# Parts of the next chunk's convolution among the copies of a turned write pass

## Chip, cores and metric

The kernel runs on one core of one Trainium2 chip, as one launch. The metric is the device time in microseconds (us); less is better. Engines are named PE (TensorE), DVE (VectorE), ACT (ScalarE), POOL (GpSimd) and SP (SyncE, which here only issues DMAs).

## What is computed

Two layers follow one another on a picture batch of 8 x 128 x 128 pixels with 128 channels. Layer 0 is a linear attention with a layer norm. Layer 1 is a two-dimensional selective scan; its first half is what this document is about. Cut to that:

```python
xz = x @ Win
xb, z = jnp.split(xz, 2, axis=-1)                 # 256 channels each
xb = conv3x3_depthwise(xb, conv_w)                # 9 taps for each channel
xb = silu(xb + conv_b)
xf = xb.reshape(Bb, Cd, L)                        # pixels in natural order
xt = transpose_of_h_and_w(xb).reshape(Bb, Cd, L)  # pixels in turned order
xs = stack([xf, xf[..., ::-1], xt, xt[..., ::-1]])
x_dbl = einsum('bcl,cd->bdl', xs_flat, Wxproj)    # 8 rows of dt, one of B, one of C
```

A scan over the 16384 pixels of each image and direction follows, and then a gate, a norm and a projection. The scan needs its input both in natural and in turned order.

## The kernel before

Three stages run one after the other: layer 0, `layer1_front` and `layer1_scan`. A barrier of all engines stands before the last. The change is in `layer1_front` alone.

**Chunks and images.** The front works on 8 images, one after the other, each in 16 chunks of 8 x 128 = 1024 pixels. The 256 channels are two halves of 128 partitions, c = 0 and c = 1. Step n handles chunk n (g is its number within the image), and parts of n + 1 and n + 2. The tile `ures` (128 x 2 x 16384, fp32) holds the whole image after the convolution; there is only one of it.

**One chunk.** For each half c:
- `project` (L476) multiplies the input with `Win` on PE into the PSUM tile `pxb`, of which there is one. `place` (L484) copies it with ACT into `xb`, with the edge columns of the neighbouring chunks.
- The nine taps of the convolution are spread over four engines. `taps_pe` (L500) does two of them, as eight matmuls into the PSUM accumulator `acc`, of which there are two. `taps_act` (L508) does three as scaled copies on ACT; POOL adds the second and the third to the first. `taps_dve` (L520) adds these three to `acc` (L522) and does the last four taps there (L524).
- `silu` (L528) writes the result from `acc` to `ures` on ACT, which frees that `acc`.

Then `rows` (L533) makes the ten rows of dt, B and C on PE, `sum_d` (L580) keeps a running sum of the directions for the skip term, `keep_rows` and `spread` (one step later) bring B to all partitions, and `by_b` (L554) multiplies the chunk in `ures` with it on DVE and writes it out in natural order.

**The write pass.** When an image is complete, `leave` (L627) writes it in turned order. It has 32 copies, k = 0 to 15 for c = 0 and k = 16 to 31 for c = 1. Each reads an eighth of the rows over all columns of `ures` into a 4 KB-per-partition tile `turned` (L635) and sends it off by a DMA of 512 KB (L636). The copies with k % 5 equal to 1 or 3 are on ACT, the others on DVE: ACT has 1, 3, 6, 8, 11, 13, 16, 18, 21, 23, 26, 28 and 31. After k = 9 and k = 19 `split` (L611) turns five of the ten rows with PE, copies them with ACT (`xh`, L619), cuts them on DVE into bf16 parts (L44, L46) and sends these off (L625). A next image's chunk can't overwrite a half of `ures` before all the copies of that half have read it.

**Buffers.** Copies with k % 3 equal to 2 use the two buffers of the tag "tc". The others use the four buffers of the tag "tb", in turn with `xh`, the two `parts` tiles of each split, the second and third tile of each `taps_act`, and `sum_d`'s tile. Each takes the buffer that the fourth allocation before it had, and waits until its last reader, mostly a DMA, is done.

**Order.** `in_order` keeps every engine's instructions, and SP's DMAs, in the order in which the program is written: an instruction that waits holds all behind it on its engine. At an image's boundary (`before and g == 0`; n = 16, 32, ... 112, and n = 128 at the end), step n has these parts: taps_dve(n,0), keep_rows, project and place of (n+1,1), taps_pe(n,1), the DMAs of load and store_sum, spread, by_b(n-1), the pass, load_sum, taps_act(n+1,0), silu(n,0), taps_pe(n+1,0), project(n+2,0), taps_dve(n,1), taps_act(n+1,1), silu(n,1), place(n+2,0), rows(n), sum_d(n). So the accumulator of (n,0) is ready before the pass and is read after it.

Of the kernel before, what the change touches and what calls it, by code (L numbers as in the profile page):

```python
# [40 lines left out]
def split3(nc, parts, x):  # L41

    for j in range(3):
        nc.vector.tensor_copy(parts[j], x)  # L44
        if j < 2:
            nc.vector.tensor_tensor(x, x, parts[j], ALU.subtract)  # L46
# [338 lines left out]
def layer1_front(ctx: ExitStack, tc, x1, win, conv_w, conv_b, wxp, d_par, ubs, xds, xps, gts, gs):  # L385
# [23 lines left out]
    def tap(dw, dh):  # L409
        return 3 * (dh + 1) + dw + 1  # L410
# [51 lines left out]
    def place_of(n):  # L462
        return SEQ[n // NCH % B], n % NCH
# [3 lines left out]
    def load(n):  # L467
        b, g = place_of(n)
        x = xins[n % 2]
        cols = CW + 1 if g < NCH - 1 else CW  # L470
        src = x1[b].rearrange("c (w h) -> c w h", h=H)[:, g * CW : g * CW + cols, :]
        nc.sync.dma_start(x[:, 0:cols, inner], src)
        if g == NCH - 1:
            nc.gpsimd.memset(x[:, CW, :], 0.0)

    def project(n, c):  # L476
        pxs[n, c] = px = pj.tile([P, CW, H], F32, name="pxb", tag="pj")
        for hf in range(2):
            nc.tensor.matmul(  # L479
                px[:, hf * 4 : hf * 4 + 4, :], wi[:, c, :], xins[n % 2][:, hf * 4 : hf * 4 + 4, inner],  # L480
                start=True, stop=True,
            )

    def place(n, c):  # L484

        g = n % NCH
        xb, old = xbs[n % 2], xbs[(n - 1) % 2]
        nc.scalar.copy(xb[:, c, 1 : CW + 1, inner], pxs.pop((n, c)))  # L488
        if g == 0:
            nc.gpsimd.memset(xb[:, c, 0, :], 0.0)  # L490
        else:
            nc.scalar.copy(old[:, c, CW + 1, inner], xb[:, c, 1, inner])
            nc.scalar.copy(xb[:, c, 0, inner], old[:, c, CW, inner])
        if g == NCH - 1:
            nc.gpsimd.memset(xb[:, c, CW + 1, :], 0.0)

    def at(n, c, dw, dh):
        return xbs[n % 2][:, c, 1 + dw : 1 + dw + CW, 1 + dh : 1 + dh + H]

    def taps_pe(n, c):  # L500
        accs[n, c] = acc = pa.tile([P, CW, H], F32, name="acc", tag="acc")
        for hf in range(2):
            s = slice(hf * 4, hf * 4 + 4)
            for j, (dw, dh) in enumerate(ON_PE):
                x = xins[n % 2][:, hf * 4 + dw : hf * 4 + dw + 4, 1 + dh : 1 + dh + H]
                nc.tensor.matmul(acc[:, s, :], wt[:, j, c, :], x, start=(j == 0), stop=(j == len(ON_PE) - 1))  # L506

    def taps_act(n, c):  # L508
        for j, d in enumerate(ON_ACT):
            if j:  # L510
                t = wp.tile([P, CW, H], F32, name="tap", tag="tb", bufs=4)
            else:
                t = wp.tile([P, CW, H], F32, name="tap", tag="ta", bufs=2)
            nc.scalar.activation(t, at(n, c, *d), AF.Copy, scale=cw[:, c, tap(*d) : tap(*d) + 1])  # L514
            if j:
                nc.gpsimd.tensor_tensor(sums[n, c], sums[n, c], t, ALU.add)  # L516
            else:
                sums[n, c] = t

    def taps_dve(n, c):  # L520
        acc = accs[n, c]
        nc.vector.tensor_tensor(acc, sums.pop((n, c)), acc, ALU.add)  # L522
        for d in ON_DVE:
            nc.vector.scalar_tensor_tensor(  # L524
                acc, at(n, c, *d), cw[:, c, tap(*d) : tap(*d) + 1], acc, ALU.mult, ALU.add
            )

    def silu(n, c):  # L528
        g = n % NCH
        u = ures[:, c, g * CH : g * CH + CH]  # L530
        nc.scalar.activation(u, accs.pop((n, c)).rearrange("p w h -> p (w h)"), AF.Silu, bias=cb[:, c : c + 1])  # L531
# [10 lines left out]
    def keep_rows(n):  # L542
        b, g = place_of(n)
        t = xdt[n % 2]
        nc.scalar.copy(t[0:64, :], prs.pop(n))
        for hf in range(2):
            s = slice(g * CH + hf * 512, g * CH + hf * 512 + 512)
            nc.sync.dma_start(xds[b][:, s], t[32 * hf : 32 * hf + R + 2, :])

    def spread(n, hf):  # L550
        pbs[n, hf] = p = pm.tile([P, 1, 512], F32, name="pb", tag="m")
        nc.tensor.matmul(p[:, 0, :], bsel[:, hf, :], xdt[n % 2], start=True, stop=True)

    def by_b(n):  # L554

        b, g = place_of(n)
        dst = ubs[b, NAT].rearrange("c p l -> p c l")
        for hf in range(2):
            s = slice(g * CH + hf * 512, g * CH + hf * 512 + 512)
            u = ures[:, :, s]  # L560
            nc.vector.tensor_tensor(u, u, pbs.pop((n, hf)).to_broadcast([P, NC2, 512]), ALU.mult)
            nc.sync.dma_start(dst[:, :, s], u)
# [8 lines left out]
    def load_sum(n, c):  # L571
        b, g = place_of(n)
        if b // 2 != 2:
            gls[n, c] = gl = wp.tile([P, CH], F32, name="gl", tag="d", bufs=2)
            if b // 2 == 0:
                nc.sync.dma_start(gl.rearrange("p (e q) -> p e q", e=NCH), gts[b % 2, c, :, :, g])
            else:
                nc.sync.dma_start(gl, sums_at(n, c))
# [21 lines left out]
    def store_sum(n, c):  # L600
        nc.sync.dma_start(sums_at(n, c), dus.pop((n, c)))
# [4 lines left out]
    def load_rows(b, i):  # L606
        r = slice(i * half, i * half + half)
        xws[b, i] = x = wp.tile([P, half, H], F32, name="xw", tag="d", bufs=2)
        nc.sync.dma_start(x, xds[b].rearrange("r (w h) -> w r h", h=H)[:, r, :])

    def split(b, i):  # L611

        r = slice(i * half, i * half + half)
        x = xws.pop((b, i))
        pt = pj.tile([P, half, P], F32, name="ptx", tag="pj")
        for j in range(half):
            nc.tensor.transpose(pt[:, j, :], x[:, j, :], ident)
        y = wp.tile([P, half, W], F32, name="xh", tag="tb", bufs=4)
        nc.scalar.copy(y, pt)  # L619
        for order, v in ((TURN, y), (NAT, x)):  # L620
            q = wp.tile([P, 3, half, P], BF16, name="parts", tag="tb", bufs=4)
            split3(nc, [q[:, j] for j in range(3)], v)
            dst = xps[b, order].rearrange("j r (a e) -> a j r e", e=P)
            for j in range(3):
                nc.sync.dma_start(dst[:, j, r, :], q[:, j])  # L625

    def leave(b):  # L627

        for i in range(2):
            load_rows(b, i)  # L630
        for k in range(NC2 * NCH):
            c, i = divmod(k, NCH)
            t = wp.tile([P, CW, W], F32, name="turned", tag="tc" if k % 3 == 2 else "tb", bufs=2 if k % 3 == 2 else 4)
            copy = nc.scalar.copy if k % 5 in (1, 3) else nc.vector.tensor_copy
            copy(t, uturn[:, c, i * CW : i * CW + CW, :])  # L635
            nc.sync.dma_start(ubs[b, TURN][c][:, i * CH : i * CH + CH], t.rearrange("p h w -> p (h w)"))  # L636
            if k % 10 == 9 and k < 20:
                split(b, k // 10)

    def step(n):  # L640

        live, then, later, before = 0 <= n < N, 0 <= n + 1 < N, 0 <= n + 2 < N, 1 <= n <= N
        b, g = place_of(n)
        if live:
            taps_dve(n, 0)
        if before:
            keep_rows(n - 1)
        if then:
            project(n + 1, 1)
            place(n + 1, 1)  # L650
        if live:
            taps_pe(n, 1)
        if later:
            load(n + 2)
        if before:
            for c in range(NC2):
                store_sum(n - 1, c)
        if live and g != 0:
            for c in range(NC2):
                load_sum(n, c)  # L660
        if before:
            for hf in range(2):
                spread(n - 1, hf)
        if before and g == 0:
            by_b(n - 1)
            leave(place_of(n - 1)[0])
        if live and g == 0:
            for c in range(NC2):
                load_sum(n, c)
        if then:  # L670
            taps_act(n + 1, 0)
        if live:
            silu(n, 0)
        if then:
            taps_pe(n + 1, 0)
        if later:
            project(n + 2, 0)
        if live:
            taps_dve(n, 1)
        if then:  # L680
            taps_act(n + 1, 1)
        if before and g != 0:
            by_b(n - 1)
        if live:
            silu(n, 1)
        if later:
            place(n + 2, 0)
        if live:
            rows(n)
            sum_d(n)  # L690
# [522 lines left out]
```

## Time and profile before

| | us |
|---|---|
| three runs: lowest, median, highest | 9591.18, 9600.28, 9600.95 |
| the profiled execution | 9596.25 |
| its span, from the first to the last instruction | 9594.5 |
| DVE busy in it | 8167.1 (85%) |
| ACT busy | 7164.4 (75%) |
| POOL busy | 7188.9 (75%) |
| PE busy | 6323.6 (66%) |

The sums over the whole span mix the stages. Cut at the stages' limits, the trace shows:

```profile
0.00:2300.00 2300.00, 2081.91 (x9222) 1280.35 (x9223) 1472.88 (x2564) 1359.70 (x2343) 1125.27 (x1255) 0.98 0.30 113
2300.00:2640.00 340.00, 302.00 (x799) 126.50 (x798) 268.57 (x240) 273.93 (x346) 198.58 (x115) 0.96 0.46 159
2640.00:4845.00 2205.00, 1640.44 (x4087) 634.19 (x4085) 1911.06 (x1654) 1741.43 (x1982) 1531.92 (x669) 0.89 0.78 255
4845.00:9594.00 4749.00, 2299.27 (x10086) 1103.17 (x10248) 4514.58 (x4211) 3789.29 (x3586) 4333.16 (x2323) 0.62 0.70 205
```

Each line is a window of the span (us from its start) and its length, then the busy time of PE, PE's weight loads, DVE, ACT and POOL with the number of instructions, and at the end the clock that TensorE was granted (1.00 is full), the share of time that the DMA engines were busy, and the GB/s that they moved. The first line is layer 0, the last the scan. The second is the start of the front up to the end of its first image, the third the rest of the front: eight write passes and seven images.

The transfers of the front that matter here, from the page (tile written and read, queue, number, size):

```profile
ubs<-ures SPq DMA_DIRECT2D x256, 512.0 KB
ubs<-turned SPq DMA_DIRECT2D x256, 512.0 KB
```

The copies of the pass have these durations in the trace: DVE x152 with a median of 1026 ns, ACT x104 with 1924 ns.

### The profile page before, as it was taken

What the parts mean: (1) busy time and instruction counts of PE and PEld (TensorE: products, weight loads), DVE (VectorE), ACT (ScalarE), POOL (GpSimd) and SP (SyncE); (2) the same over time, 40 slices, a digit from 0 to 9 for tenths busy, and PEclk for the clock granted to TensorE, in tenths of its full rate; (3) what the DMA queues carried; (4) which work ended last, traced back from release to release, by engine and by line L of the source; (5) the groups of instructions that cost most, each with busy time, mean ns of one, the idle gap of its engine ahead of it and who ended that gap; (6) DMA issues with size and microseconds to landing.
All of it is one profiled execution on the core that took longest, in us unless ns stands there. A gap on an engine that the chain in (4) does not pass through costs nothing. (4 is left out here: it accounts for less than half of the span.)

```text
span 9594.5 us, 89820 instructions
## 1 busy us (share of the span) xinstructions
PE 6323.6 (66%) x24190; PEld 3144.2 (33%) x24352; DVE 8167.1 (85%) x8668; ACT 7164.4 (75%) x8256; POOL 7188.9 (75%) x4361
## 2 busy tenths in 40 slices
PE   8999998988977788777823544636345363543636
PEld 5555655554322233222300311304023040220403
DVE  6667765563988899888989999999999999999996
ACT  5556565566877788777878888887887888788785
POOL 3445544455665578776859999998998999999897
PEclk9999999999988899888955755757556575665857
DMA  2332233313476678987765957769486685867858
GB/s 91 133 133 83 92 132 132 132 75 135 172 262 233 227 262 248 266 264 265 248 199 166 271 164 216 229 177 263 150 237 203 185 259 164 242 190 198 242 165 212
DMA packets 1034807, 1851.21 MB, mean 193 GB/s; under 512 B 274852, under 2 KB 500772, under 8 KB 1026112
## 3 DMA queue, kind: packets, MB, share of 16 engines
q1 hardware_dynamic: 999488, 1711.23, 54.2%
q0 software_dynamic: 34816, 134.23, 7.1%
q8 instruction: 199, 3.26, 0.1%
q14 instruction: 304, 2.49, 0.1%
HBM read 1153.03 MB, written 692.12 MB: 192 GB/s over the span
## 5 line engine op out<-in xcount | busy, mean ns | idle before, releaser
L892 POOL TENSOR_TENSOR ubt<-ubt,sp 128x1024 f32<-128x1024 f32 x1024 | 2457.5, 2456 | 197.3 <-ACT sp L885 107.8
L881 PE MATMUL px<-rows,dtw 128*128 128x512 bf16 x1893 | 914.6, 576 | 2259.8 <-DVE y L951 1032.6
L516 POOL TENSOR_TENSOR tap<-tap 128x1024 f32<-128x1024 f32 x512 | 1206.0, 2366 | 634.7 <-ACT tap L514 511.8
L524 DVE SCALAR_TENSOR_TENSOR acc<-xb,cw,acc 128x1024 f32<-128x1024 f32 x1024 | 1320.7, 1290 | 52.7 <-ACT tap L514 0.9
L885 ACT ACTIVATE sp<-px 128x1024 f32<-128x1024 f32 x1024 | 1044.2, 1024 | 398.3 <-PE px L881 244.5
L958 POOL TENSOR_TENSOR y<-y,ubt 128x512 f32<-128x512 f32 x768 | 1164.2, 1568 | 138.0 <-DVE ubt L932 135.1
L506 PE MATMUL acc<-xi,wt 128*128 128x512 f32 x2048 | 953.9, 609 | 384.6 <-ACT ures L531 384.2
L881 PEld LDWEIGHTS <-dtw 128*128 128x128 bf16 x2048 | 164.8, 110 | 3054.1 <-issue 951.5
L889 ACT ACTIVATE px<-sp,sa 128x1024 f32<-128x1024 f32 x1024 | 1110.2, 1109 | 6.1
L899 DVE TENSOR_TENSOR_SCAN ubt<-px,state,ubt 128x1024 f32<-128x1024 f32 x480 | 1106.2, 2336 | 6.6 <-issue 4.9
L901 DVE TENSOR_TENSOR_SCAN ubt<-px,state,ubt 128x1024 f32<-128x1024 f32 x480 | 1105.0, 2336 | 6.5 <-issue 4.7
L514 ACT ACTIVATE tap<-xb,cw 128x1024 f32<-128x1024 f32 x768 | 834.0, 1139 | 68.4 <-POOL tap L516 67.9
L885 ACT ACT_TABLE_LOAD x512 | 656.9, 1283 | 185.3 <-PE px L881 149.8
L282 POOL TENSOR_TENSOR q<-q,qs 128x512 f32<-128x512 f32 x256 | 271.2, 1060 | 642.2 <-DVE qs L281 642.2
L506 PEld LDWEIGHTS acc<-xi,wt 128*128 128x128 f32 x2048 | 383.9, 192 | 929.8 <-ACT ures L531 486.7
L889 ACT ACT_TABLE_LOAD x512 | 656.9, 1283 | 9.1
L1023 PEld LDWEIGHTS px<-wg,z 128*128 128x128 f32 x4096 | 586.7, 229 | 132.2 <-issue 126.4
L1023 PE MATMUL px<-wg,z 128*128 128x128 f32 x4096 | 585.6, 312 | 0.0
L915 PE MATMUL pc<-rows,csel 128*128 128x512 bf16 x1017 | 516.3, 588 | 100.8 <-DVE rstd L1011 91.8
L479 PE MATMUL pxb<-xi,wi 128*128 128x512 f32 x1024 | 495.9, 606 | 4.3 <-ACT xb L488 4.3
L951 DVE TENSOR_TENSOR y<-y,px 128x1024 f32<-128x1024 f32 x384 | 468.6, 1220 | 14.2
L298 ACT ACTIVATE sq<-o 128x512 f32<-128x512 f32 x256 | 161.2, 630 | 423.0 <-DVE o L296 421.8
(158 smaller groups left out, 15369.2 us busy)
## 6 DMA issues: line engine op xcount, KB each, us to landing
ubt<-ubs SPq DMA_DIRECT2D x512, 1024.0 KB
zs<-z SPq DMA_DIRECT2D x512, 256.0 KB
ubs<-ures SPq DMA_DIRECT2D x256, 512.0 KB
ubs<-turned SPq DMA_DIRECT2D x256, 512.0 KB
z<-zs SPq DMA_DIRECT2D x256, 512.0 KB
y<-gs POOLq DMA_DIRECT2D x128, 1024.0 KB, 12.0
rows<-xps SPq DMA_DIRECT2D x1536, 60.0 KB
xi<-x SPq DMA_DIRECT2D x120, 576.0 KB
```

Source lines behind the costliest of these rows:

```text
L506: nc.tensor.matmul(acc[:, s, :], wt[:, j, c, :], x, start=(j == 0), stop=(j == len(ON_PE) - 1))
L514: nc.scalar.activation(t, at(n, c, *d), AF.Copy, scale=cw[:, c, tap(*d) : tap(*d) + 1])
L516: nc.gpsimd.tensor_tensor(sums[n, c], sums[n, c], t, ALU.add)
L524: nc.vector.scalar_tensor_tensor(acc, at(n, c, *d), cw[:, c, tap(*d) : tap(*d) + 1], acc, ALU.mult, ALU.add)
L881: nc.tensor.matmul(p[:, hf * 512 : hf * 512 + 512], sl.dw[:, c * P : c * P + P], src, start=True, stop=True)
L885: nc.scalar.activation(t, da[n, c], AF.Softplus)
L889: nc.scalar.activation(da[n, c], sp[n, c], AF.Exp, scale=sa[:, sl.s, c : c + 1])
L892: nc.gpsimd.tensor_tensor(ubt[n][:, c, :], ubt[n][:, c, :], sp.pop((n, c)), ALU.mult)
L899: nc.vector.tensor_tensor_scan(e[:, ::-1], x[:, ::-1], e[:, ::-1], start, ALU.mult, ALU.add)
L901: nc.vector.tensor_tensor_scan(e, x, e, start, ALU.mult, ALU.add)
L958: nc.gpsimd.tensor_tensor(v[:, c], v[:, c], h[:, c], ALU.add)
L1023: nc.tensor.matmul(po[:, w, :], z[:, c, w * H : w * H + H], wg[:, c, :], start=(c == 0), stop=(c == NC2 - 1))
```

## The change

The parts from taps_act(n+1,0) to taps_act(n+1,1) no longer come after the pass at an image's boundary. They are handed to `leave` as a table, and `leave` calls them among its copies: silu(n,0), taps_act(n+1,0) and taps_pe(n+1,0) after copy 15, taps_dve(n,1) after copy 22, project(n+2,0) after copy 23 and taps_act(n+1,1) after copy 25. Within a boundary silu(n,0) now stands ahead of taps_act(n+1,0). All other steps keep their order, written as branches of their own, but for load_sum of the very first step, which loads nothing (image 4 has no sum to load). After the last image the table is empty.

```diff
-    def leave(b):
+    def leave(b, meanwhile):
...
             if k % 10 == 9 and k < 20:
                 split(b, k // 10)
+            for todo in meanwhile.get(k + 1, []):
+                todo()
...
         if before and g == 0:
             by_b(n - 1)
-            leave(place_of(n - 1)[0])
+            meanwhile = {}
+            if live:
+                meanwhile = {16: [lambda: silu(n, 0)], 23: [lambda: taps_dve(n, 1)]}
+                if then:
+                    meanwhile[16] += [lambda: taps_act(n + 1, 0), lambda: taps_pe(n + 1, 0)]
+                    meanwhile[26] = [lambda: taps_act(n + 1, 1)]
+                if later:
+                    meanwhile[24] = [lambda: project(n + 2, 0)]
+            leave(place_of(n - 1)[0], meanwhile)
+        elif live:
+            if then:
+                taps_act(n + 1, 0)
+            silu(n, 0)
+            if then:
+                taps_pe(n + 1, 0)
+            if later:
+                project(n + 2, 0)
+            taps_dve(n, 1)
+            if then:
+                taps_act(n + 1, 1)
+            if before:
+                by_b(n - 1)
...
         if live and g == 0:
             for c in range(NC2):
                 load_sum(n, c)
-        if then:
-            taps_act(n + 1, 0)
-        if live:
-            silu(n, 0)
...
-        if before and g != 0:
-            by_b(n - 1)
```

More of the change, by code (lines that the diff above doesn't have):

```diff
@@ L665, in step @@
             by_b(n - 1)
-            leave(place_of(n - 1)[0])
+            meanwhile = {}
[20 more added lines that the diff above has]
+                by_b(n - 1)
+        elif n < 0:
+            if then:
+                taps_act(n + 1, 0)
+                taps_pe(n + 1, 0)
+            project(n + 2, 0)
+            if then:
+                taps_act(n + 1, 1)
         if live and g == 0:
@@ L669, in step @@
                 load_sum(n, c)
-        if then:
-            taps_act(n + 1, 0)
-        if live:
-            silu(n, 0)
[L674 to L681, printed above, removed]
-        if before and g != 0:
-            by_b(n - 1)
         if live:
```

## The prediction

> **What bounds the kernel now.** I read the page first (sums by stage), then the busy time by window around one turned write pass, then the timeline of each engine there. The pass shown is the second of eight, at the step n = 32.
>
> ```profile
> 2950.00:3006.00 56.00, 2.63 (x10) 1.86 (x10) 34.31 (x43) 26.44 (x16) 0.00 (x0) 0.51 0.97 359
> 3006.00:3021.00 15.00, 10.88 (x26) 4.22 (x27) 9.01 (x8) 12.27 (x14) 9.39 (x4) 0.77 0.32 125
> 3036.00:3051.00 15.00, 14.15 (x37) 5.36 (x36) 14.58 (x13) 13.77 (x18) 9.43 (x4) 1.00 0.54 183
> ```
> Columns: window, length, busy us of PE, PEld, DVE, ACT, POOL, then TensorE clock, DMA share, GB/s. Two regimes are to be seen. In the chunk loop (last line) DVE works 14.58 of 15 us: it is the bound. In the pass (first line) DMA is at 0.97 and DVE (34 of 56 us) and ACT (26 of 56) wait for it. The middle line is the restart: DMA 0.32 and DVE 9.0 of 15, so nothing is full there. This is what the change can win, seven times (the eighth pass has no next chunk).
>
> ```profile
> 2975.01 3.83 DVE L635 COPY turned<-ures 128x1024 f32<-128x1024 f32 x4
> ...
> 2993.19 3.83 DVE L635 COPY turned<-ures 128x1024 f32<-128x1024 f32 x4
> 2998.35 1.03 DVE L635 COPY turned<-ures 128x1024 f32<-128x1024 f32 x1 [1.34 <-DMA ubs<-turned]
> ...
> 3003.14 1.23 DVE L522 TENSOR_TENSOR acc<-tap,acc 128x1024 f32<-128x1024 f32 x1
> 3004.40 5.27 DVE L524 SCALAR_TENSOR_TENSOR acc<-xb,cw,acc 128x1024 f32<-128x1024 f32 x4
> 3015.38 1.23 DVE L522 TENSOR_TENSOR acc<-tap,acc 128x1024 f32<-128x1024 f32 x1 [5.71 <-PE acc L506]
> 3016.65 5.33 DVE L524 SCALAR_TENSOR_TENSOR acc<-xb,cw,acc 128x1024 f32<-128x1024 f32 x4
> 3024.26 1.23 DVE L522 TENSOR_TENSOR acc<-tap,acc 128x1024 f32<-128x1024 f32 x1 [2.28 <-PE acc L506]
> ```
> DVE's timeline: start, length, instruction, and in brackets its idle time and what ended it. The three L522 are taps_dve(n,1), (n+1,0) and (n+1,1). From 3024.26 on DVE has no gaps, so **the measure of everything below is when taps_dve(n+1,1) starts**.
>
> ```profile
> 2978.78 1.92 ACT L635 COPY turned<-ures 128x1024 f32<-128x1024 f32 x1 [2.60 <-DMA ubs<-turned]
> 2981.42 1.92 ACT L635 COPY turned<-ures 128x1024 f32<-128x1024 f32 x1 [0.72 <-DMA ubs<-turned]
> 2985.40 0.69 ACT L619 COPY xh<-ptx 128x640 f32<-128x640 f32 x1 [2.06 <-DMA ubs<-turned]
> ...
> 3003.92 1.93 ACT L635 COPY turned<-ures 128x1024 f32<-128x1024 f32 x1 [2.34 <-DMA ubs<-turned]
> 3005.76 3.31 ACT L514 ACTIVATE tap<-xb,cw 128x1024 f32<-128x1024 f32 x3
> 3008.98 1.09 ACT L531 ACTIVATE ures<-acc,cb 128x1024 f32<-128x1024 f32 x1
> ...
> 3013.90 1.09 ACT L531 ACTIVATE ures<-acc,cb 128x1024 f32<-128x1024 f32 x1
> ```
> ACT ends the pass with copy 31 (3003.92); only then come three taps, silu(n,0), three taps, silu(n,1).
>
> ```profile
> 3010.12 5.12 PE L506 MATMUL acc<-xi,wt 128*128 128x512 f32 x8 [41.90 <-ACT ures L531]
> 3015.08 1.88 PE L479 MATMUL pxb<-xi,wi 128*128 128x512 f32 x4
> 3016.89 1.91 PE L540 MATMUL pr<-ures,wx 128*32 128x512 f32 x8
> 3018.73 1.99 PE L479 MATMUL pxb<-xi,wi 128*128 128x512 f32 x4
> 3020.55 3.60 PE L506 MATMUL acc<-xi,wt 128*128 128x512 f32 x8
> ```
> PE has idled for 42 us, is cold (5.12 us against 3.60 warm for the same eight matmuls; 6.76 at the first boundary), and hands DVE its two accumulators.
>
> Copy 31 to taps_dve(n+1,1) is thus 3024.26 - 3003.92 = 20.3 us here; over the seven boundaries 20.3 to 21.9, mean **21.4 us**.
>
> **What the Trainium skill says.** "TensorE: Matmul & The Clock Gate", section "What's actually happening": an idle PE falls to half clock and needs some 3.4 us of work to come back, in a free-running window. The trace agrees: clock 0.50 in the pass, eight matmuls in 5.1 to 6.8 us after it. "DMA: Bandwidth & Descriptors", section "Anatomy of one DMA — SWDGE (gpsimd) path", gives a fixed 2.0 us plus bytes over 436 GB/s (for GpSimd's path; these transfers are SyncE's), so 3.2 us as an estimate for 512 KB. The trace has 2.72 us from issue to the buffer's next owner when the queue was empty (issue 2976.06, copy 2978.78) and 1.3 us for each further one; I use these. "Perfetto Trace Analysis", section "Optimization Strategy", says that interleaving two regimes may help; the trace decides whether the waiting regime has room.
>
> **The change, part by part.** Nothing is added or removed in work; no moved part issues a DMA, and SP's order of transfers stays (load_sum still behind the 32 writes). For each boundary:
>
> Moved into the pass, after copy 15: silu(n,0) 1.1 + three taps 3.3 us on ACT, two adds of 2.4 on POOL (idle there), eight matmuls on PE (cold, up to 6.8 us). After copy 22: taps_dve(n,1), 6.5 us of DVE. After copy 23: project(n+2,0) on PE, hidden. After copy 25: three more taps on ACT, two POOL adds. Each trio takes two of the four "tb" buffers that the copies turn through.
>
> Walk of the new pass, by the order in the queues, with each copy after its buffer's last reader:
> - silu(n,0) follows DVE's copy 15 at 2978.9, the taps end at 2983.2. Copies 16 and 18 (ACT) move from 2978.8 and 2981.4 to 2983.2 and 2985.3. The transfers of copies 10 to 15 last until 2985.3, so DMA loses only 1.3 us.
> - PE does the cold matmuls 2980.1 to 2986.9, and the transposes of the second split stand behind them: done at 2988.2, not before 2985. xh on ACT ends at 2989 (2986.1 before), so the split on DVE starts about 2.1 us later and ends at 2995.2.
> - DVE copies 20 and 22 until 2997.0, then taps_dve(n,1) until 3003.5. Copies 24 and 25, which ran by 2997.0, now end at 3005.5. The writes of 20 to 23 last until about 3003, so DMA runs dry.
> - ACT's second taps wait for taps_dve(n,1)'s first instruction (2998.2) and for the writes of copies 21 and 22; they end near 3002.6 and their POOL adds at 3006.1: hidden under DVE's block.
> - Copy 24's write lands 2.7 us after its issue, 3007.3; 25's at 3008.6. Copy 28 (ACT) takes 25's buffer: 3008.6 to 3010.5. Copy 31 starts at **3010.5** against 3003.9: the pass is 6.6 us longer.
>
> I take 6.6 to 7.3 us (the higher one with the split 0.8 later). What sets it is DVE's block and the fact that a drained queue costs a round trip.
>
> Saved after copy 31: the two tap trios (6.5 us with waits), silu(n,0) and the cold matmuls are gone from the path. Left are: copy 1.9, silu(n,1) 1.1, then on PE rows(n), project(n+2,1), taps_pe(n+1,1), warm 1.9 + 2.0 + 3.6. PE is cold now at this place instead, as its cover has moved into the pass: rows doubles to 3.8, project is half cold, 2.9. With 0.1 for hand-overs: 1.9 + 1.1 + 3.8 + 2.9 + 3.6 + 0.1 = **13.4 us**. DVE begins taps_dve(n+1,0) near 3010.4 instead of 3015.4, but is done at 3017 and waits for PE.
>
> Sum: 21.4 - 13.4 = 8.0 us saved, 6.6 to 7.3 lost: about 1 us gained for each boundary, seven times, **7 us**. The profiled execution took 9596.25 us (span 9594.5), hence 9589; the median of the three runs shown is 4 us above it. For a median I take 9592.
>
> Bounds of what the trace doesn't show: the length of the pass with taps in it lies between +0 (all hidden under DMA) and +11 (the whole delay of copy 24, 8.4 us, and one more round trip of 2.7). The cold PE at the new place costs 0 to 5.5 us (all of rows and project at half clock is 3.9, with part of taps_pe 5.5); I took 2.8.
>
> **The rivals.**
> *The pass hides most of it.* The queue holds more than I count or DVE's block lands where copies wait anyway; the pass grows by half of my 7 us or not at all. For it: DVE idles 22 of 56 us there. Against: these gaps are 1.3 us each between copies, and a 6.5 us block doesn't fit. Gain 4.5 to 8 us each, 31 to 56 us: 9540 to 9565.
> *The drained queue decides (slower).* Place: the last eight copies. Two of four buffers are with the taps, so each later copy waits for a write just three or four before it, with the 2.7 us trip. If copy 31 slips the full 11 us, each boundary loses 3: 9596 + 21, about 9617 to 9621. It decides once the pass grows by over 8.0 us. For it: copy 24's delay of 8.4 us is itself over this, and only the queue's backlog softens it. Against: the walk, in which copies 26 and 29 take the other pair of buffers ("tc"), free long before.
> *The parts don't interleave,* as a wait holds ACT before copy 16: silu(n,0) needs copy 15 alone, which is done in time, so I give this little.
>
> **How the numbers follow.** What a measurement of this kernel can tell from no change is about 0.2%, 19 us, or 2.7 us for each boundary. Near zero: 0.52, 9573 to 9611. Hidden: 0.28. Drained queue: 0.20. Range: 9558 to 9618, which leaves out the best of the second and the worst of the third. Faster 0.29, same 0.51, slower 0.20.
>
> **What would show it.** Right: between copy 23's and copy 24's write a gap on SP, with DVE in L524; the last copy some 7 us later after the pass's start; L540 as the first matmuls after the pass and at twice its time; DVE waiting some 6 us for PE before taps_dve(n+1,1). Wrong: a pass of unchanged length (then the gain is near 8 us each), ACT waiting for POOL's adds before copy 30 or 31, or DVE gaps later in the chunk loop.

## The result, and the profile after

The time is the same: 9594.08 us median against 9591.68 us, 12 runs each, ratio 1.0002 with a 95% interval of 0.9993 to 1.001. The profiled execution took 9598.29 us (span 9596.5). Lines of the file below the change have moved; the copies of the pass are L636 here and their DMAs L637.

The second boundary again. The first copy starts at 2951.41 (2950.72 before), so the windows are moved by 0.7 us. Columns: window, length, busy us of PE, PEld, DVE, ACT, POOL, then TensorE clock, DMA share, GB/s.

```profile
2950.70:3006.70 56.00, 10.70 (x26) 4.58 (x26) 34.55 (x42) 29.94 (x20) 8.27 (x4) 0.63 0.86 316
3006.70:3021.70 15.00, 5.91 (x12) 2.04 (x13) 11.82 (x9) 10.06 (x11) 1.83 (x1) 0.57 0.72 283
```

PE, ACT and POOL now work within the pass, but the DMA share there fell from 0.97 to 0.86, and the writes go on into the restart (0.72 after 0.32). Work was put into the pass, and the pass became longer.

DVE's timeline in the changed kernel:

```profile
2987.81 1.03 DVE L636 COPY turned<-ures 128x1024 f32<-128x1024 f32 x1 [5.83 <-POOL tap L516]
...
2998.59 1.22 DVE L522 TENSOR_TENSOR acc<-tap,acc 128x1024 f32<-128x1024 f32 x1
2999.85 5.26 DVE L524 SCALAR_TENSOR_TENSOR acc<-xb,cw,acc 128x1024 f32<-128x1024 f32 x4
3005.02 7.21 DVE L636 COPY turned<-ures 128x1024 f32<-128x1024 f32 x5
3012.16 1.21 DVE L522 TENSOR_TENSOR acc<-tap,acc 128x1024 f32<-128x1024 f32 x1
3013.41 5.33 DVE L524 SCALAR_TENSOR_TENSOR acc<-xb,cw,acc 128x1024 f32<-128x1024 f32 x4
3024.05 1.23 DVE L522 TENSOR_TENSOR acc<-tap,acc 128x1024 f32<-128x1024 f32 x1 [5.32 <-PE acc L506]
```

The block of taps_dve(n,1) runs at 2998.59 between copies 22 and 24. The five copies of the x5 are 24, 25, 27, 29 and 30. The last L522 is taps_dve(n+1,1), the prediction's measure: it starts 72.6 us after the first copy (73.5 before).

ACT's timeline at the two trios of taps and at the pass's end:

```profile
2980.72 3.22 ACT L514 ACTIVATE tap<-xb,cw 128x1024 f32<-128x1024 f32 x3
2985.37 3.84 ACT L636 COPY turned<-ures 128x1024 f32<-128x1024 f32 x2 [1.43 <-POOL tap L516]
...
2999.84 1.15 ACT L514 ACTIVATE tap<-xb,cw 128x1024 f32<-128x1024 f32 x1 [3.27 <-DVE acc L522]
3001.85 2.44 ACT L514 ACTIVATE tap<-xb,cw 128x1024 f32<-128x1024 f32 x2 [0.85 <-DMA ubs<-turned]
3004.19 1.93 ACT L636 COPY turned<-ures 128x1024 f32<-128x1024 f32 x1
3008.56 1.94 ACT L636 COPY turned<-ures 128x1024 f32<-128x1024 f32 x1 [2.45 <-POOL tap L516]
3012.66 1.93 ACT L636 COPY turned<-ures 128x1024 f32<-128x1024 f32 x1 [2.16 <-DMA ubs<-turned]
```

Copies 16 and 28 here, and copy 19 in DVE's lines above (2987.81), wait for POOL: the copies right behind a trio get the trio's two buffers, and these come free only after POOL's adds. (The description above, by which each takes the buffer of the fourth allocation before it, doesn't hold at these places.) Copy 31 starts at 3012.66, 61.2 us after the first copy. It doesn't wait for POOL: the semaphore that releases it is that of copy 25's write, here and in the kernel before. So the end of the pass depends on when copy 25 is done. SP's queue, POOL and copy 25 on DVE:

```profile
2997.77 2.88 SPq L637 DMA_DIRECT2D ubs<-turned  x4
3006.35 9.70 SPq L637 DMA_DIRECT2D ubs<-turned  x8
```
```profile
3003.07 5.46 POOL L516 TENSOR_TENSOR tap<-tap 128x1024 f32<-128x1024 f32 x2 [15.29 <-ACT tap L514]
```
```profile
3006.25 3.17 DVE L636 COPY turned<-ures 128x1024 f32<-128x1024 f32 x1
```

Between the writes of copies 23 and 24 SP issues nothing for 5.7 us, as DVE is in its block. Then copy 25 takes 3.17 us instead of 1.03: POOL's second add runs from 3005.51 to 3008.53, and the copy ends 0.89 us after it. The same happens at each of the seven boundaries (the last section has more on it).

PE's timeline:

```profile
2991.76 1.05 PE L540 MATMUL pr<-ures,wx 128*32 128x512 f32 x4
3015.79 1.92 PE L540 MATMUL pr<-ures,wx 128*32 128x512 f32 x4 [22.98 <-ACT ures L531]
3017.64 2.87 PE L479 MATMUL pxb<-xi,wi 128*128 128x512 f32 x4
3020.35 3.60 PE L506 MATMUL acc<-xi,wt 128*128 128x512 f32 x8
```

Half of rows(n) runs within the pass; the other half is the first work after it, cold (1.92 us against 1.05 us for as many matmuls).

Means over the seven boundaries, in us after the pass's first copy on DVE. The third L522 is taps_dve(n+1,1), the fifth is taps_dve(n+2,1), one step later. The last column is the time from the first pass's first copy to the eighth's, which holds all seven boundaries.

```
                         copy 31   third L522   fifth L522   first to eighth pass
before                      53.0         74.4         89.6                 2145.2
after                       60.6         72.6         89.3                 2141.5
block alone                 55.7         76.7         92.0                 2158.4
block behind                55.7         71.8         87.1                 2124.4
block early                 58.8         70.6         87.5                 2127.6
sums early                  60.7         72.3         87.5                 2127.3
second trio out             58.4         70.3         92.0                 2161.2
block early, trio out       55.5         67.4         88.7                 2138.1
all moved                   57.0         68.9         90.8                 2154.3
all moved, PE warm          57.2         68.7         89.9                 2146.6
first trio ahead            56.4         68.3         84.7                 2110.7
... two sums early          57.1         69.1         84.3                 2109.6
```

The changed kernel gains 1.8 us at the third L522 and has 0.3 us of it left at the fifth. The difference is at two boundaries. At the fourth (n = 64, image 0) the fifth L522 comes at 96.1 us (89.4 before), at the fifth (image 1) at 90.8 (89.7). The fourth boundary in the changed kernel, DVE, POOL and SP:

```profile
3634.61 1.23 DVE L522 TENSOR_TENSOR acc<-tap,acc 128x1024 f32<-128x1024 f32 x1 [5.27 <-PE acc L506]
...
3646.23 1.23 DVE L522 TENSOR_TENSOR acc<-tap,acc 128x1024 f32<-128x1024 f32 x1 [2.77 <-POOL tap L516]
...
3657.81 1.23 DVE L522 TENSOR_TENSOR acc<-tap,acc 128x1024 f32<-128x1024 f32 x1 [4.98 <-PE acc L506]
```
```profile
3635.77 5.68 POOL L593 TENSOR_TENSOR du<-du,gl 128x1024 f32<-128x1024 f32 x2 [16.64 <-ACT tap L514]
3641.39 9.55 POOL L516 TENSOR_TENSOR tap<-tap 128x1024 f32<-128x1024 f32 x4
```
```profile
3616.95 9.70 SPq L637 DMA_DIRECT2D ubs<-turned  x8
3626.74 5.99 SPq L576 DMA_DIRECT2D gl<-gts  x2
```

ACT had its part of the sums ready from 3628 on (`du`, L589, starts 3627.21). POOL adds them to the tile `gl` from 3635.77 only, though nothing else was on it, and the label "ACT tap" names an instruction long done. What came late is `gl`: SP issues its reads behind the 32 writes, at 3626.74, here 65.0 us after the first copy against 56.7 before. POOL's adds for the next taps stand behind these sums, and DVE waits for them. At the other boundaries with sums the reads are as late (64.1 to 64.7 us after the first copy), but POOL starts 6.2 to 6.5 us after their issue, against 9.0 and 7.3 at the fourth and fifth, and DVE doesn't wait.

### The profile page after: what moved, and what is told of

Its sections match the earlier page's. It is cut to its first block, busy times and chain, and to the rows that moved or that the text cites. A ratio compares the mean times of both kernels' runs of the same rounds, so it can differ in the third digit from the quotient of the medians.

```text
span 9596.5 us, 89946 instructions
## 1 busy us (share of the span) xinstructions
PE 6383.4 (67%) x24352; PEld 3148.8 (33%) x24352; DVE 8183.6 (85%) x8668; ACT 7166.6 (75%) x8256; POOL 7193.6 (75%) x4361
## 5 line engine op out<-in xcount | busy, mean ns | idle before, releaser
L898 PE MATMUL px<-rows,dtw 128*128 128x512 bf16 x2048 | 954.1, 566 | 2219.4 <-DVE y L968 1032.6
L524 DVE SCALAR_TENSOR_TENSOR acc<-xb,cw,acc 128x1024 f32<-128x1024 f32 x1024 | 1320.3, 1289 | 52.7 <-DVE acc L524 0.9
```

The source lines that it names most:

```text
L524: nc.vector.scalar_tensor_tensor(acc, at(n, c, *d), cw[:, c, tap(*d) : tap(*d) + 1], acc, ALU.mult, ALU.add)
L898: nc.tensor.matmul(p[:, hf * 512 : hf * 512 + 512], sl.dw[:, c * P : c * P + P], src, start=True, stop=True)
```

## The experiments

Each ratio is to the kernel before. Three rounds each unless five are named.

**1. DVE's block alone, in the kernel before.**

```diff
-            leave(place_of(n - 1)[0])
+            leave(place_of(n - 1)[0], {23: [lambda: taps_dve(n, 1)]} if live else {})
...
-        if live:
+        if live and not (before and g == 0):
             taps_dve(n, 1)
```

> The kernel before, with one part of the change alone: taps_dve(n,1) after copy 22, all else behind the pass as it was. My theory: DVE's block of 6.5 us drains the write queue, so copy 31 starts 6 to 7 us later after the pass's first copy than the 52.8 to 53.2 us of before at the second boundary, and nothing is saved, since ACT and PE set the restart: 6 to 7 us lost at each of 7 boundaries, ratio about 1.0045. Rival (the block hides under the queued writes and the gain is eaten elsewhere): the pass is unchanged, ratio 1.000.

Measured: 1.0024 (1.0014 to 1.0033). Copy 31 moves by 2.7 us, the fifth L522 by 2.3. SP's queue at the last 12 writes, in the kernel before and in this one:

```profile
2994.24 13.01 SPq L636 DMA_DIRECT2D ubs<-turned  x12
```
```profile
2998.39 16.17 SPq L636 DMA_DIRECT2D ubs<-turned  x12
```

The block does cost, but 2.7 us and not the 6 to 7 expected. Copy 25's write is issued 52.5 us after the first copy instead of 47.9, and copy 31 starts 3.2 us after that issue instead of 5.1: the emptier queue gives back part of the delay. Both statements fell in part: it isn't hidden, and it isn't the one cause of a pass that is 7.6 us longer.

**2. The block and the second trio behind the pass.**

```diff
-                meanwhile = {16: [lambda: silu(n, 0)], 23: [lambda: taps_dve(n, 1)]}
+                meanwhile = {16: [lambda: silu(n, 0)], 32: [lambda: taps_dve(n, 1)]}
...
-                    meanwhile[26] = [lambda: taps_act(n + 1, 1)]
+                    meanwhile[32] += [lambda: taps_act(n + 1, 1)]
```

> The changed kernel with taps_dve(n,1) and the second trio of taps put back behind copy 31; silu(n,0), the first trio, taps_pe and project stay in the pass. My theory: without DVE's block the pass grows only by ACT's trio and the late split, 2 to 3 us, while some 6 of the 10 us saved behind copy 31 stay saved: 3 us gained at each boundary, ratio about 0.998. Rival (ACT's trio and the buffers that it takes lengthen the pass, not DVE's block): copy 31 still comes 6 us or more late, and with the second trio behind it again each boundary loses 1 to 2 us, ratio 1.001.

Measured: 0.9984 (0.9978 to 0.9991). Copy 31 at 55.7, the first trio with silu and taps_pe thus costs 2.6 us, and 2.6 us are gained at the fifth L522. The delay is there in full when the second split ends (45.3 us after the first copy, 42.7 before). The theory's numbers hold, the rival's don't.

**3. The block after copy 5.**

```diff
-                meanwhile = {16: [lambda: silu(n, 0)], 23: [lambda: taps_dve(n, 1)]}
+                meanwhile = {16: [lambda: silu(n, 0)], 6: [lambda: taps_dve(n, 1)]}
```

> The changed kernel with one number changed: taps_dve(n,1) after copy 5 instead of after copy 22. There DVE has an idle stretch of 8 us in any case, waiting for the first write to land. My theory: the block is free there; the pass grows by 2 to 3 us (ACT's first trio) instead of 6 to 9, and what follows copy 31 stays at 11.5 us: 7 us gained at each boundary, less what the late sums cost at the fourth one, ratio about 0.995. Rival (what costs is the work in the pass, wherever it stands, or the buffers): ratio 1.000, copy 31 as late as in the changed kernel.

Measured: 0.9986 (0.9979 to 0.9993). The direction held, the size didn't: copy 31 at 58.8, third L522 at 70.6, and the two late sums stay. The pass is 5.8 us longer than before, where 2 to 3 were expected; what follows copy 31 takes 11.8 us, as expected. DVE and ACT at the pass's end in this kernel:

```profile
3000.03 5.06 DVE L636 COPY turned<-ures 128x1024 f32<-128x1024 f32 x3 [4.92 <-POOL tap L516]
```
```profile
3003.30 3.79 ACT L636 COPY turned<-ures 128x1024 f32<-128x1024 f32 x2 [2.58 <-POOL tap L516]
3005.14 1.94 ACT L636 COPY turned<-ures 128x1024 f32<-128x1024 f32 x1
```

ACT's first line holds copies 28 and 31, the second copy 31 alone. (The 56.9 us that the expectations of 6 and 9 give for copy 31 in this kernel is the start of copy 28.) With the block gone from the end of the pass, copy 27 waits 4.9 us and copy 28 2.6 us for POOL: the second trio's buffers are the next limit. In the changed kernel part of this wait lies behind the block.

**4. The sums' reads after copy 23.**

```diff
-        if live and g == 0:
+        if live and g == 0 and not before:
             for c in range(NC2):
                 load_sum(n, c)
...
+                meanwhile.setdefault(24, []).extend([lambda: load_sum(n, 0), lambda: load_sum(n, 1)])
```

> The changed kernel with the two reads of load_sum(n) issued after copy 23 instead of behind all 32 writes. At the fourth boundary of the changed kernel POOL starts these sums 9 us after ACT has its part ready, and DVE then waits 2.8 us for POOL and 5.0 us for PE. My theory: the reads are late because the pass ends late; here POOL starts with ACT's part, the two waits go, 7 to 8 us are gained at the fourth boundary, perhaps some at the fifth, and the ratio to before is about 0.999, in which the profile tells more than the time. Rival (POOL's own length, not the reads, causes the waits): both waits stay.

Measured: 0.9988 (0.9981 to 0.9995). The fifth L522 at the fourth and fifth boundary comes at 87.2 and 86.5 instead of 96.1 and 90.8, 13.2 us in all; copy 31 stays at 60.7. POOL at the fourth boundary starts with ACT's part:

```profile
3620.49 5.68 POOL L593 TENSOR_TENSOR du<-du,gl 128x1024 f32<-128x1024 f32 x2 [9.51 <-ACT du L589]
```

So the late reads, not POOL's length, made DVE wait. 13 us are 0.14% of the time, which is the step from 1.0002 to 0.9988.

**5. The second trio alone taken out of the pass.**

```diff
-                    meanwhile[26] = [lambda: taps_act(n + 1, 1)]
...
         if later:
             place(n + 2, 0)
+        if then and before and g == 0:
+            taps_act(n + 1, 1)
```

> The changed kernel with the second trio of taps alone taken out of the pass, to stand behind place(n+2,0), where ACT and POOL have 8 us before DVE needs it; DVE's block stays after copy 22. Theory now: the pass of the changed kernel is 7.4 us longer because of three parts of about 2.5 us each (first trio, block, second trio with the two buffers it takes). So copy 31 starts near 58 us after the first copy instead of 60.5, and taps_dve(n+1,1) at about 70 instead of 72.5: ratio about 0.9975. Rival (the second trio is hidden behind the block, as the prediction's walk had it): copy 31 stays at 60 and the ratio at 1.000.

Measured: 1.0013 (1.0006 to 1.002), slower. Copy 31 (58.4) and the third L522 (70.3) came as the theory said; the fifth didn't, at 92.0. ACT's and DVE's timelines at the second boundary:

```profile
3018.46 3.23 ACT L514 ACTIVATE tap<-xb,cw 128x1024 f32<-128x1024 f32 x3
3023.11 1.15 ACT L589 ACTIVATE du<-ures,sd 128x1024 f32<-128x1024 f32 x1 [1.43 <-POOL tap L516]
3025.54 1.15 ACT L589 ACTIVATE du<-ures,sd 128x1024 f32<-128x1024 f32 x1 [1.28 <-POOL tap L516]
```
```profile
3026.35 1.23 DVE L522 TENSOR_TENSOR acc<-tap,acc 128x1024 f32<-128x1024 f32 x1 [6.49 <-PE acc L506]
...
3038.32 1.23 DVE L522 TENSOR_TENSOR acc<-tap,acc 128x1024 f32<-128x1024 f32 x1 [3.11 <-PE acc L506]
...
3047.20 1.23 DVE L522 TENSOR_TENSOR acc<-tap,acc 128x1024 f32<-128x1024 f32 x1 [2.28 <-PE acc L506]
```

The trio and two waits for POOL stand between place(n+2,0) and the next step's place on ACT: from 3018.46 to 3027.06, 8.6 us, against 3.5 us in the changed kernel (3017.08 to 3020.55). The accumulators come later for the two halves after, and DVE waits three times instead of once. On PE, taps_pe(n+2,0) waits 3.6 us for silu(n+1,0), which now comes later on ACT, and after this pause it runs slower (5.40 us against 3.70 in the changed kernel):

```profile
3032.78 5.40 PE L506 MATMUL acc<-xi,wt 128*128 128x512 f32 x8 [3.59 <-ACT ures L531]
```

The theory had looked at the third L522 alone. DVE runs without gaps only if ACT keeps its lead of the next step as well; the fifth L522 is the better measure.

This run also shows what the second trio costs in the changed kernel. Up to copy 24 both passes are alike (it starts 53.2 us after the first copy here and 53.3 there). But DVE's five copies behind the block take 4.83 us here and 7.21 there, and copy 25 ends at 55.2 instead of 57.8:

```profile
3008.53 4.83 DVE L636 COPY turned<-ures 128x1024 f32<-128x1024 f32 x5
```

So beside the block the second trio lengthens the pass by way of POOL's adds, which hold up DVE's copies.

**6. The block early and the second trio out.** Experiments 3 and 5 together.

> As the kernel with the block after copy 5, and with the second trio behind place(n+2,0). Theory: with both out of the pass's end only the first trio is left, copy 31 at 55.5 us after the first copy (56.9 with the second trio in the pass), DVE's last copies no longer stretched by POOL's adds, and taps_dve(n+1,1) at 67.5 to 68 instead of 70.5 (74.4 in the kernel before): ratio about 0.996. Rival (PE's restart sets it, not the buffers): copy 31 comes earlier but taps_dve(n+1,1) stays at 70.

Measured: 0.9994 (0.9986 to 1.0003). Copy 31 at 55.5 and the third L522 at 67.4, as expected; the fifth at 88.7. Against experiment 3 the pass gains 3.3 us by the trio's leaving (58.8 to 55.5) and the third L522 3.2, but the fifth comes 1.2 us later: the restart loses it all, the trio standing at the same place on ACT as in experiment 5.

**7. All moved.** As 6, with the first trio ahead of by_b, taps_pe behind the second split, the sums' reads after copy 23:

```diff
         if before and g == 0:
+            if live and then:
+                taps_act(n + 1, 0)
             by_b(n - 1)
...
+                    meanwhile.setdefault(20, []).extend([lambda: taps_pe(n + 1, 0)])
+                meanwhile.setdefault(24, []).extend([lambda: load_sum(n, 0), lambda: load_sum(n, 1)])
```

> In addition the first trio ahead of by_b(n-1), where ACT idles 5.1 us before the first copy, taps_pe(n+1,0) after copy 19 so that the transposes of the second split no longer stand behind it, and the reads of load_sum after copy 23. Theory: the pass is then as long as in the kernel before but for silu(n,0), copy 31 at 53 to 54, taps_dve(n+1,1) at 65.5 to 66 against 74.4, no wait for the sums at the fourth boundary: 8 us for each of seven, ratio about 0.994. Rival: what the trio takes of buffers and POOL at the pass's start costs as much as at its old place, copy 31 stays at 55.5: ratio 0.996.

Measured: 1.0012 (1.0005 to 1.0018), a miss. At the second boundary, whose image has no sums to read, copy 31 comes at 53.1, as expected; at the six others at 56.5 to 58.9. SP's queue at the third boundary:

```profile
3297.38 2.88 SPq L637 DMA_DIRECT2D ubs<-turned  x4
3300.35 2.41 SPq L578 DMA_DIRECT2D gl<-gts  x2
3302.85 10.72 SPq L637 DMA_DIRECT2D ubs<-turned  x8
```

The reads of 1 MB stand ahead of the last eight writes. In experiment 4 the DMA engines had idle time there (share 0.55 from 3305 to 3310) and copy 31 didn't move; here they are full (0.99 in the same window) and all eight writes come later. With the second trio's place added, the gain is gone.

**8. The same with a warm PE.**

```diff
+            if k == 29 and meanwhile:
+                w = pm.tile([P, 512], F32, name="warm", tag="m")
+                for j in range(4):
+                    nc.tensor.matmul(w, ident, t.rearrange("p h w -> p (h w)")[:, 0:512], start=True, stop=True)
```

> The same with four matmuls of no use on copy 29's tile (their result is not read), so that PE has worked for some 5 us when rows(n) comes. Theory: PE's cold restart costs about 2 us at each boundary (rows of the second half 1.9 instead of 1.0 us, project 2.9 to 3.7 instead of 2.0, but the first half's rows, 1.0 us, now stand behind the extra matmuls): 1 to 2 us gained at each boundary, ratio to before lower by 0.001 than without. Rival (PE's clock is hidden by DVE's or ACT's own work): no difference, or a loss of the 1 us.

Measured: 1.0011 (1.0003 to 1.0019), as without. Copy 31 to the third L522 takes 11.5 us instead of 11.9. Yet PE itself gained what the theory said. At six of the seven boundaries the first half of rows(n) is still done ahead of the second, and PE has the accumulator ready 9.6 us after copy 31's start instead of 11.6 to 12.0. (At the second boundary all of rows(n) runs behind the extra matmuls, and hardly anything is gained.) The first boundary, PE and DVE:

```profile
2710.81 3.60 PE L506 MATMUL acc<-xi,wt 128*128 128x512 f32 x8
```
```profile
2716.36 1.23 DVE L522 TENSOR_TENSOR acc<-tap,acc 128x1024 f32<-128x1024 f32 x1 [5.25 <-POOL tap L516]
```

PE is done at 2714.41, but DVE waits until 2716.36, now for POOL's adds of the second trio, which stands behind place in this kernel. So the cold clock costs PE some 2 us at a boundary, and here the next wait in line hides it. In the changed kernel and in 9 these adds are done within the pass and DVE waits for PE; whether a warm PE pays there wasn't run.

**9. First trio ahead, second left in the pass (five rounds).** Experiment 3, and of 7 the first trio and taps_pe alone.

> From the kernel with the block after copy 5: the first trio goes ahead of by_b(n-1), where ACT idles 5.1 us, and taps_pe(n+1,0) behind the second split; the second trio stays after copy 25 and the sums' reads stay behind the pass. Theory: the first trio costs 2.5 us at its old place (it holds ACT's copies 16 and 18, and two buffers) and almost nothing ahead of the pass: copy 31 at 54 to 55 us after the first copy instead of 56.9, the third L522 at 68, the fifth at 83.5 to 84 instead of 85.8 (89.6 in the kernel before); the late sums of the fourth and fifth boundary stay. Ratio to before about 0.997. Rival (the second trio alone sets the end of the pass, through the buffers that it takes): copy 31 stays at 56.5 to 57 and the ratio at 0.9986.

Measured: 0.9973 (0.9962 to 0.9984), 9565.88 us median. Copy 31 at 56.4, third L522 at 68.3, fifth at 84.7 (82.7 to 85.0 but for 88.5 at the fourth boundary). DVE at the second boundary:

```profile
2999.18 1.22 DVE L522 TENSOR_TENSOR acc<-tap,acc 128x1024 f32<-128x1024 f32 x1
...
3011.70 1.23 DVE L522 TENSOR_TENSOR acc<-tap,acc 128x1024 f32<-128x1024 f32 x1 [5.93 <-PE acc L506]
...
3020.46 1.22 DVE L522 TENSOR_TENSOR acc<-tap,acc 128x1024 f32<-128x1024 f32 x1
```

The first copy is at 2943.18, so the one remaining wait ends 68.5 us after it, and none follows. Against experiment 3 copy 31 comes 2.4 us earlier, which is the 2.5 us that the theory gave the first trio; its 54 to 55 us started from the 56.9 that belong to copy 28. At copy 22's end the pass is now as in the kernel before (44.4 and 44.6 us after the first copy). The 3.4 us by which it is still longer arise after that, where the second trio stands.

**10. The same with the reads of images 0 and 1 early (five rounds).**

```diff
+                if b < 2:
+                    meanwhile.setdefault(24, []).extend([lambda: load_sum(n, 0), lambda: load_sum(n, 1)])
```

> The same, and the sums' reads after copy 23 for images 0 and 1 only, whose reads are strided. Theory: at these two boundaries copy 31 comes 2 to 4 us later, as the reads stand ahead of eight writes, but the later waits of DVE for POOL and PE (8 and 4 us in the changed kernel) go; 4 to 6 us gained in all, ratio about 0.9965. Rival (POOL is full in these images and makes DVE wait in any case): the fifth L522 at these boundaries stays at 90 to 93 us and the time is the same or worse.

Measured: 0.9967 (0.9954 to 0.998), 9557.18 us median, the fastest of all; its interval overlaps that of 9. At the two boundaries copy 31 comes 1.7 us later than in 9, the fifth L522 at 85.7 and 85.4 instead of 88.5 and 85.0: 2.4 us in sum, less than the 4 to 6 expected.

## Why the prediction was right, point by point

**The bound and the measure.** Right. The pass was bound by DMA, and the time followed DVE's gaps. The measure was one step too short: at the fourth boundary the loss came after taps_dve(n+1,1).

**The longer pass.** Forecast 6.6 to 7.3 us, measured 7.6 (copy 31 at 60.6 against 53.0). The total nearly held, its share among the parts didn't. The prediction put nearly all on DVE's block and held the second trio's adds to be "hidden under DVE's block". The runs show 2.7 us for the block alone (1) and 2.6 for the first trio with silu and taps_pe (2); with both, and without the second trio, the pass is 5.3 us longer (5), which is their sum. The second trio adds 2.2 us beside the block (after against 5), and 3.3 without it (3 against 6), so only 1 us of it is hidden. The step that was wrong is the time of copies 24 and 25: the walk gave them 2.0 us right behind the block, and the trace has 4.5, as they wait for POOL's adds. Copy 25's write was thought to land at 3008.6, 57.9 us after the first copy, and to release copy 28; in the trace it lands at 61.1 and releases copy 31. That the total came out near was in part luck.

**What is left behind copy 31.** Forecast 13.4 us, measured 12.0 (72.6 - 60.6). The mis-sized term is rows(n), put at 3.8 us: its first half needs only silu(n,0), so it ran within the pass (L540 at 2991.76), and 1.92 us were left. PE was cold as the prediction said ("TensorE: Matmul & The Clock Gate", section "What's actually happening"): project took 2.87 us here, where 2.9 were forecast.

**The sum.** Forecast 1 us for each boundary, 7 in all. At the third L522 it is 1.8 us, 12.6 in all; from the first pass to the eighth 3.7 us are left (2145.2 - 2141.5). The loss is at the fourth and fifth boundary: between the third and the fifth L522 they lose 8.0 and 2.6 us against the kernel before. This was not in the working: it said that SP's order stays and stopped there. The order did stay, but the reads of the sums stand behind the writes and so moved with the pass's end. Moved forward alone (4), they gave 13 us. So the forecast of the median, 9592 us against 9594 measured, is closer than the working deserves: the gain behind copy 31 was larger than forecast, and a loss that was not forecast took most of it. Without that loss (4, 0.9988) the time would still have been in the range.

**The rivals.** "Hides most of it" is out, as the pass grew by its full amount. "The drained queue decides" named the right place, the last eight copies, but the pass would have had to grow by more than was saved: 8.0 us by the prediction's sum, 9.4 by the measured one (21.4 - 12.0), and it grew by 7.6. The third is out: silu(n,0) came in time.

**The signs.** All four for "right" are there: the gap of 5.7 us on SP between the writes of copies 23 and 24, a last copy 7.6 us later, L540 first after the pass and at nearly twice its time, and DVE's wait for PE (5.3 us) before taps_dve(n+1,1). But one of those for "wrong" is there too, DVE's gaps later in the chunk loop, at the fourth and fifth boundary.

What stays open: why copies 16 and 19 get the trio's buffers while others get older ones wasn't looked into further, and the first trio's 2.6 us weren't divided among ACT, buffers and the later transposes on PE.

## What to carry to other kernels

In this pass, which waits for DMA, the engines were idle but the buffers weren't, and work put into it was free only at some places. taps_dve(n,1) cost 2.7 us among short gaps, and nothing to be seen in DVE's 8 us gap near the start (copy 31 at 55.5 us with it there, 55.7 with it behind the pass). The first trio cost 2.6 us after copy 15 and nothing to be seen ahead of the pass. So look for one long gap of the engine, for work that takes no buffer that the transfers turn through, and for what else runs at that time: an add on an idle POOL held up the copies on DVE.

When the end of such a stage moves, list what its DMA queue issues behind it, as these reads move too. Check the engine that follows for two steps, not to the first work that starts earlier. And when a shortened part brings no time, look at which wait ends last now: in experiment 8 PE gained 2 us and POOL was next in line.

## What the runs showed of the hardware

By the figures, DVE's turned copies and POOL's adds took turns. In the front of the twelve traces 77 of these copies start while an add runs. Each of them ends 0.88 to 0.90 us after that add's end, and so takes up to 3.20 us instead of 1.02. In 30 other cases the copy starts first, by 0.04 to 0.06 us. Then the copy keeps its 1.03 us and the add is the one that waits: it ends 2.20 to 2.22 us after the copy and takes up to 3.19 us instead of 2.37. In the kernel before no add falls beside a copy of the pass, and no copy is over 1.08 us; the same holds where the second trio isn't in the pass and the first stands at its old place (experiments 2, 5, 6). The chunk loop's L522 and L524 show nothing of this: they take 1.22 and 1.29 us with and without POOL beside them. "GPSIMD Engine Reference", section "Key points", says that GpSimd shares its SBUF interfaces with VectorE, with contention for DVE instructions in a 2-port mode or with two SBUF inputs. The copies have one input, so the first of these would have to be their case; no run here shows in which mode they ran.
